# A graph-attention layer on one core: a sixth pair's rows gathered from x, and four moves in the schedule

## The chip, the core and the metric

The kernel runs on one core of a Trainium2 chip. The metric is the device time of one execution in microseconds. A core has five engines that work through their own instruction streams: TensorE (PE; its weight loads are shown as PEld), VectorE (DVE), ScalarE (ACT), GpSimd (POOL) and SyncE (SP). They wait for each other by semaphores. Here SP issues nearly all plain transfers, POOL issues the gathers, and ACT issues a few loads of edge attributes.

## The reference

For 12500 nodes and 400000 edges, sorted by target node `dst`, all in float32:

```python
h = relu(layernorm(x))                                  # 12500 x 128
msg_src = h @ w_src + b_src;  msg_dst = h @ w_dst
message = msg_src[src] + msg_dst[dst]                   # 400000 x 128
rad = silu(silu(edge_attr @ w1 + b1) @ w2 + b2) @ w3 + b3   # 32 -> 64 -> 64 -> 128
message = message * edge_weight * rad
message = message @ w_sep + b_sep                       # 128 -> 256: 8 heads x (16 alpha, 16 value)
alpha = 0.6*a + 0.4*a*(2*sigmoid(a) - 1)                # a: the alpha half
score = sum over k of alpha * alpha_dot                 # one per edge and head
att = softmax of score over the edges of each target
out = segment_sum(value * att, dst) @ w_proj + b_proj
return x + out
```

## The kernel before

**Node phase** (some 110 us). The 98 tiles of 128 rows of x are held in SBUF and handled in quads of four tiles. A first loop over 25 quads makes the layer norm, the transposes (`turn`) and the product with `w_src`, and stores the table `t_src` in DRAM. A second loop (28 rounds in both versions) makes the product with `w_dst` (`products(i, 1)`) and stores the table `t_dst`. Both tables wait for copies from PSUM by ACT, and SP stores them. Into the second loop other work is laid by round number (`extra`): `spans`, `cuts`, `direct_ids`, `spreads`, and four `marks` (L601, DVE), which compare neighbouring targets and end with four stores to `same`. SP takes one load of weights or of first edge data per round from a list (`weights_list`).

**Raw sections.** A section is 512 edges, a pair of sections is 1024 edges, and there are 391 pairs. `t_src` can be gathered from only once it is whole. So for the first `RAW` pairs POOL gathers rows of x itself (`raw_gather`, L381), right at the start; in the second loop these rows get their own statistics (`raw_roots`, L390), layer norm (`raw_norm`, L406 and L408), transposes and relu (`raw_turn`, L416), a quad of four tiles at a time, and later PE multiplies them by `w_src` (`sources`, L1169) instead of turning gathered rows of `t_src` (L1173).

**Windows phase** (the rest). The scheduling is by hand: each engine runs its instructions in the order in which the Python code emits them. `step(k)` for k = -5 to 390 issues stages of several pairs at once:

- loads on SP: the target rows `md` of pair k+4 (`load_md`, L1080), `dst` (`load_d`, L187), edge weights of pair k+2 (`load_w`, L194); edge attributes on ACT's queue for the first pairs, then on SP's (L175)
- `split_md(k+1, 0)` on ACT (L1090) and `split_md(k+1, 1)` on DVE (L1094): the target rows of the pair, made into the stationary operand of `message`
- `alphas(k-1, f)`, f = 0 and 1: PE (L1197), then a Silu on ACT (L1199), then `alphas_sum` on DVE (L1204)
- `sources(k, f)` on PE, `gather(k+2, f)` on POOL (L1111: four gathers of 128 rows, eight per pair)
- the radial network: `mlp1(k+2)` (PE L1127, two Silu on ACT L1130, out of half of the bank `misc` and half of the bank `m`), `mlp2(k+1)` (PE L1140, ACT L1142), `mlp3(k)` (PE L1157) and `radial(k)` (DVE L1162)
- `one_hot_T(k+1)`: two ACT instructions (L1151, L1152) make the one-hot matrix of the targets
- `message(k)`: PE (L1186), then DVE (L1191) writes `mT`, the product with `rad`
- every second step `scores` of two pairs (PE L1214, into the bank `m`)
- from step 8 on, the softmax of eight pairs, spread over steps: at k % 8 == 3 an Exp on ACT (`softmax_exp`, L1250, with a table load before it and one before the next Silu), the copy S (L1218) and two rounds of transposes with ACT copies into `Pem` (`softmax_T`, L1284, L1287)
- from step 12 on (`LAG`) the values of pair k-12 (PE L1325, DVE L1327), the one-hot sums (L1340, L1352) and their stores.

Buffers: `mT` and `early` are one ring of 13 pairs. In the node phase slots 10, 11 and 12 of it hold the first edge weights, the first `dst` rows and the second edge weights; slots 0 to 4 hold raw rows; gathers of pairs 5 to 12 go into `early`, pair 10 only when `message(0)` has used the weights there. Pairs 13 to 18 have six buffers `gs`, pair 19 borrows two others, pair 20 takes the buffer of pair 13 again, and from pair 26 on each pair takes that of six pairs before. `padded_rows` loads four blocks of x, adds a bias and stores them, one half per step in steps 40 to 47.

Of the kernel before, what the change touches and what calls it, by code (L numbers as in the profile page):

```python
# [43 lines left out]
MP = 8  # L44
MQ = 2 * MP
LAG = 12
RAW = 5
# [10 lines left out]
def gnn_kernel(ctx: ExitStack, tc: tile.TileContext, a: dict, out: bass.AP):  # L58
# [139 lines left out]
    with tc.tile_pool(name="node1", bufs=1) as n1, tc.tile_pool(name="node", bufs=2) as np_, \  # L198
# [80 lines left out]
        def weights_list():  # L279

            pairs = []
            first = ("heads", "dot", "b_v", "w_proj", "b_proj", "b_a")
            for name, t in sorted(wt.items(), key=lambda v: v[0] not in first):
                ap = a[name]
                if name == "b_src":
                    ap = ap.rearrange("o c -> c o")
                elif name == "b_proj":
                    ap = ap.to_broadcast([P, C])
                pairs.append((t, ap))
            for f in range(2):  # L290
                for q in range(2):
                    o = (2 * q + f) * RAD
                    pairs.append((w1b[o:o + RAD, f * FC:(f + 1) * FC], a["fc_w1"]))
                s = slice(f * FC, (f + 1) * FC)
                for q in range(2):
                    pairs.append((w2b[s, q * FC:(q + 1) * FC], a["fc_w2"]))
                pairs += [(w3b[s, :], a["fc_w3"]), (b12[s, 0:1], a["fc_b1"]), (b12[s, 1:2], a["fc_b2"])]
            return [lambda t=t, ap=ap: nc.sync.dma_start(out=t, in_=ap) for t, ap in pairs] + \
                [lambda k=k: load_e(k, nc.sync) for k in range(4)] + \
                [lambda: load_d(0, early[AHEAD - 2].bitcast(I32).rearrange("p (n e) -> p n e", n=2)),  # L300
                 lambda: load_w(0, early[AHEAD - 3]), lambda: load_w(1, early[AHEAD - 1])]
# [336 lines left out]
        roots(quads[3][0], quads[4][1])  # L638
        more = iter(weights_list())
        limits = load_limits()  # L640
        for i in range(Q):
# [31 lines left out]
            if i == 19:  # L673
                ends_load()
        extra = {7: lambda: (spans(), places()), 10: cuts, 12: direct_ids, 14: spreads,
                 15: lambda: marks(0), 16: lambda: marks(1), 18: lambda: marks(2), 20: lambda: marks(3)}
        for i in range(2 * RQ + 8):
            if i < Q:
                products(i, 1)
            if i % 2 == 0 and 0 <= i // 2 - 4 < RQ:  # L680
                raw_turn(i // 2 - 4)
            q = i // 2 - 1
            if i % 4 == 2 and q < RQ:
                raw_roots(q, q + 2)
            if i % 4 == 3 and q < RQ:
                raw_scales(q, q + 2)
            if i % 2 == 0 and 0 <= q - 1 < RQ:
                raw_norm(q - 1)
# [5 lines left out]
            if i == 2 * RQ:  # L694
                nc.scalar.activation(silu, eps[0:1, :], AF.Silu)
# [313 lines left out]
    def windows():  # L1009
# [7 lines left out]
        with tc.tile_pool(name="ps", bufs=1, space=PSUM) as pp, \  # L1017
# [104 lines left out]
            def mlp1(k):  # L1122
# [6 lines left out]
                for f in (1, 0):  # L1129
                    nc.scalar.activation(h1s[k][:, f, :], p1[f], AF.Silu, bias=b12[:, 0:1], scale=1.0)  # L1130
# [510 lines left out]
            for k in range(2):  # L1641
                load_md(k)

# [20 lines left out]
            def step(k):  # L1664
# [31 lines left out]
                if 0 <= k - 40 < 8:  # L1696
                    padded_rows(k - 40)
# [10 lines left out]
                if has(k + 1) and k >= 0:  # L1708
                    split_md(k + 1, 0)
# [3 lines left out]
                if k == NP:  # L1713
                    tail_head(c)
                    return
                if has(c):
# [12 lines left out]
                if has(k + 1) and k >= 0:  # L1729
                    split_md(k + 1, 1)  # L1730
# [9 lines left out]
                if has(k + 2):  # L1740
                    mlp1(k + 2)
                if has(k + 1):
                    one_hot_T(k + 1)
                if has(k):
                    radial(k)
                if k == 0:
                    for i in range(2):
                        split_md(0, i)
# [30 lines left out]
                if has(k + 2):  # L1779
                    gather(k + 2, 1)  # L1780
                if has(k + 3):
# [11 lines left out]
                if has(k):  # L1793
                    message(k)
                if has(k - MP) and r == 3:
# [230 lines left out]
```

## Time and profile before

| | us |
|---|---|
| median of 3 runs | 4045.88 |
| lowest, highest | 4044.23, 4051.89 |
| the profiled execution | 4045.58 |
| its span, first to last instruction | 4043.7 |
| PE busy | 3734.2 |
| POOL busy | 3015.5 |
| DVE busy | 2966.2 |
| ACT busy | 2317.5 |

A row of the timeline gives the start and the duration in us, the engine, the line of the code, the operation, output and input, the count, and in brackets the idle time of the engine before it with what ended it. A row of the groups gives line, engine, operation, shapes and count, then busy time and mean ns of one, then the idle time before them and what ended most of it. A row of the windows gives busy time (and instructions) of PE, PEld, DVE, ACT and POOL, then the granted clock, the busy share of the DMA engines and GB/s. POOL's time between two gathers is not booked as busy: issuing instructions do not count. The mean granted TensorE clock was 0.974.

### The profile page before, as it was taken

The page shows a single profiled execution, that of the slowest core. Times are in us where ns is not written, and L with a number is a line of the kernel's source. Part 1 is how long each engine was busy: PE and PEld are TensorE (multiplying, and loading weights), DVE is VectorE, ACT ScalarE, POOL GpSimd, SP SyncE. Part 2 cuts the span into 40 slices and gives each one's busy share as a digit, 9 for nine tenths or more (in the row PEclk, how much of TensorE's full clock was granted, in tenths as well). Part 3 has the DMA queues.
Part 4 walks back from the last instruction along what each step waited for, and adds up shares of the span by engine and source line. Part 5 has one row for each costly group of instructions (what it writes and reads, how often), then busy time and mean ns, then how long its engine had stood idle before and what let it go on. Part 6 is the DMA issues. An engine that isn't in the chain of part 4 may idle for free. (4 is left out here: it accounts for less than half of the span.)

```text
span 4043.7 us, 82719 instructions
## 1 busy us (share of the span) xinstructions
PE 3734.2 (92%) x27186; PEld 2198.2 (54%) x27186; DVE 2966.2 (73%) x5236; ACT 2317.5 (57%) x4463; POOL 3015.5 (75%) x3193
## 2 busy tenths in 40 slices
PE   7699999999999999999999999999999999999997
PEld 6255555555555555555555555555555555565555
DVE  8477777777777767677777677777777777777876
ACT  7565555666655556555655565555555555555561
POOL 6767777777777777777777777777777777777776
PEclk9899999999999999999999999999999999999998
DMA  8756666666666665665566666666666666666662
GB/s 256 189 154 166 166 177 170 162 171 170 175 160 170 167 162 159 166 162 166 158 169 169 163 164 169 168 162 165 172 171 159 178 167 180 174 179 181 174 166 56
DMA packets 435839, 678.82 MB, mean 168 GB/s; under 512 B 96574, under 2 KB 268510, under 8 KB 435291
## 3 DMA queue, kind: packets, MB, share of 16 engines
q1 hardware_dynamic: 331931, 464.59, 39.4%
q0 software_dynamic: 101888, 207.34, 21.8%
q8 instruction: 220, 3.60, 0.4%
q14 instruction: 216, 1.77, 0.2%
q10 hardware_dynamic: 1584, 1.51, 0.1%
HBM read 620.73 MB, written 54.06 MB: 167 GB/s over the span
## 5 line engine op out<-in xcount | busy, mean ns | idle before, releaser
L1111 POOL DMA_INDIRECT gs<-t_src,idx x3013 | 2849.4, 946 | 932.4 <-issue 757.2
L1204 DVE SCALAR_TENSOR_TENSOR al<-pa,sl 128x512 f32<-128x512 f32 x781 | 538.9, 690 | 544.1 <-ACT sl L1199 533.2
L1197 PE MATMUL pa<-mT,c_w_a 128*128 128x512 f32 x1562 | 884.1, 648 | 38.7 <-DVE mT L1191 17.9
L1199 ACT ACTIVATE sl<-pa,c_b_a 128x512 f32<-128x512 f32 x781 | 536.8, 687 | 666.4 <-PE pa L1197 659.5
L1325 PE MATMUL V<-c_w_v,mT 128*128 128x128 f32 x6154 | 891.2, 288 | 11.4 <-DVE pvx L1327 10.7
L1325 PEld LDWEIGHTS V<-c_w_v,mT 128*128 128x128 f32 x6154 | 757.3, 194 | 240.9 <-issue 186.3
L1173 PEld LDWEIGHTS pm<-ident,gs 128*128 128x128 f32 x3013 | 374.5, 143 | 536.3 <-issue 526.3
L1142 ACT ACTIVATE h<-p,b 128x512 f32<-128x512 f32 x391 | 467.7, 1196 | 345.7 <-PE p L1140 339.5
L1327 DVE TENSOR_TENSOR pvx<-V,Pem 128x512 f32<-128x512 f32 x770 | 528.0, 686 | 146.4 <-PE V L1325 96.9
L1162 DVE SCALAR_TENSOR_TENSOR w_b<-p,c_fc_b,w_b 128x1024 f32<-128x1024 f32 x389 | 498.2, 1281 | 147.1 <-PE p L1157 119.7
L1173 PE MATMUL pm<-ident,gs 128*128 128x128 f32 x3013 | 464.3, 277 | 99.5 <-DMA gs<-t_src,idx 98.9
L1191 DVE SCALAR_TENSOR_TENSOR mT<-pm,c_b_src,w_b 128x1024 f32<-128x1024 f32 x389 | 495.6, 1274 | 14.8 <-PE pm L1186 14.5
L1130 ACT ACTIVATE h<-misc,b 128x256 f32<-128x256 f32 x391 | 185.6, 475 | 540.7 <-PE misc L1127 522.4
L1157 PE MATMUL p<-h,w3b 64*128 64x512 f32 x1564 | 454.9, 659 | 8.0 <-ACT h L1142 8.0
L1197 PEld LDWEIGHTS pa<-mT,c_w_a 128*128 128x128 f32 x1562 | 236.2, 191 | 288.3 <-issue 78.7
L1214 PE MATMUL m<-al,w_s 128*32 128x512 f32 x1564 | 215.8, 623 | 80.8 <-ACT h L1130 79.6
L1152 ACT ACTIVATE ohT<-d_b,ones 128x512 fp32r<-128x512 f32 x389 | 280.8, 722 | 13.0
L1151 ACT ACTIVATE d_b<-d_b,tgt 128x512 f32<-128x512 int32 x389 | 279.9, 719 | 0.0
L1140 PE MATMUL p<-h,w2b 64*64 64x256 f32 x3128 | 260.3, 403 | 0.0
L1127 PEld LDWEIGHTS m<-eT,w1b 64*128 64x128 f32 x782 | 151.0, 193 | 196.6 <-issue 169.9
L1127 PE MATMUL m<-eT,w1b 64*128 64x256 f32 x782 | 239.5, 387 | 3.9 <-DMA t_dst<-ms 2.7
L1127 PE MATMUL misc<-eT,w1b 64*128 64x256 f32 x782 | 239.5, 387 | 0.0
(257 smaller groups left out, 3730.3 us busy)
## 6 DMA issues: line engine op xcount, KB each, us to landing
w_b<-in_edge_weight SPq DMA_DIRECT2D x388, 512.0 KB
d_b<-in_dst SPq DMA_DIRECT2D x388, 256.0 KB
e_t<-in_edge_attr SPq DMA_DIRECT2D x381, 128.0 KB
gs<-t_src,idx POOLq DMA_INDIRECT x3013
md<-t_dst SPq DMA_DIRECT2D x782, 32.0 KB
win<-ob SPq DMA_DIRECT2D x230, 68.0 KB
agg<-ob SPq DMA_DIRECT2D x640, 16.5 KB
xs<-in_x SPq DMA_DIRECT2D x26, 256.0 KB
```

The source lines that it names most:

```text
L1111: sent = [nc.gpsimd.indirect_dma_start(out=gs[:, t, :], out_offset=None, in_=t_src[:, :], in_offset=bass.IndirectOffsetOnAxis(ap=idx[:, t0 ...
L1127: nc.tensor.matmul(p1[f], w1b[s, :], eTs[k][s, :], start=True, stop=True)
L1142: nc.scalar.activation(h2s[k].rearrange("x (h i b) -> x h b i", h=2, b=2 * TS), p2[:, :, 0:2 * T].rearrange("x h (b i) -> x h b i", b=2 * TS),
L1157: nc.tensor.matmul(p3[:, f, 0:SEC], w3b[s, :], h2s[k][s, :], start=True, stop=True)
L1162: nc.vector.scalar_tensor_tensor(rad[:, 0:n], p3.rearrange("c f e -> c (f e)")[:, 0:n], b3, rad[:, 0:n], op0=ALU.add, op1=ALU.mult)
L1173: turned = [nc.tensor.matmul(pm[:, t * T:(t + 1) * T], gs[:, t, :], ident, start=(t == 0), stop=False, is_transpose=True, skip_group_check ...
L1191: nc.vector.scalar_tensor_tensor(mTs[k][:, 0:n], pms.rearrange("c f e -> c (f e)")[:, 0:n], b_n, rad[:, 0:n], op0=ALU.add, op1=ALU.mult)
L1197: nc.tensor.matmul(pa[:, 0:n], w_a, mTs[k][:, f * SEC:f * SEC + n], start=True, stop=True)
L1199: nc.scalar.activation(sl[:, 0:n], pa[:, 0:n], AF.Silu, bias=b_a, scale=1.0)
L1204: nc.vector.scalar_tensor_tensor(al, pa, 0.25, sl, op0=ALU.mult, op1=ALU.add)
L1325: nc.tensor.matmul(V[:, t, :], mTs[c][:, o:o + T], w_v, start=True, stop=True)
L1327: nc.vector.tensor_mul(pvx[c][:, f, 0:n, 0:C].rearrange("p t (h k) -> p t h k", h=H), V[:, 0:n, :].rearrange("p t (h k) -> p t h k", h=H), ...
```

## The change

1. `RAW` is 6 instead of 5: 48 raw gathers instead of 40, 12 raw quads instead of 10, and 8 gathers from `t_src` fewer.
2. The raw work of a round becomes a function `raw_rows`. Its first four rounds run in the last four rounds of the first loop, beside the four `marks`, which move there too from rounds 15 to 20 of the second loop. The second loop keeps its 28 rounds.
3. The second pair's edge weights are no longer in the list of the node phase: `load_w(1)` is issued by SP behind the first two `load_md`.
4. In step 0 the target rows of pair 0 are split at the usual place, and those of pair 1 behind `message(0)`; before, pair 1 came first.
5. `one_hot_T(k+1)` moves behind the second alphas, sources and gathers of its step, in every step.
6. In steps with k % 8 == 3 from 11 on, `mlp1(k+2)` moves to the same place, so that it is behind the second alphas. For odd pairs below 320 its two Silu change order.
7. The eight halves of `padded_rows` are spread over steps 40 to 51.

```diff
-RAW = 5
+RAW = 6
@@ weights_list
-                 lambda: load_w(0, early[AHEAD - 3]), lambda: load_w(1, early[AHEAD - 1])]
+                 lambda: load_w(0, early[AHEAD - 3])]
@@ node phase
+        def raw_rows(i):
+            if i % 2 == 0 and 0 <= i // 2 - 4 < RQ:
+                raw_turn(i // 2 - 4)
+            q = i // 2 - 1
+            if i % 4 == 2 and q < RQ:
+                raw_roots(q, q + 2)
+            if i % 4 == 3 and q < RQ:
+                raw_scales(q, q + 2)
+            if i % 2 == 0 and 0 <= q - 1 < RQ:
+                raw_norm(q - 1)
...
+            if 0 <= i - (Q - 4) < 4:
+                marks(i - (Q - 4))
+                raw_rows(i - (Q - 4))
-        extra = {7: lambda: (spans(), places()), 10: cuts, 12: direct_ids, 14: spreads,
-                 15: lambda: marks(0), 16: lambda: marks(1), 18: lambda: marks(2), 20: lambda: marks(3)}
-        for i in range(2 * RQ + 8):
+        extra = {7: lambda: (spans(), places()), 10: cuts, 12: direct_ids, 14: spreads}
+        for i in range(2 * RQ + 4):
             if i < Q:
                 products(i, 1)
...
+            raw_rows(i + 4)
...
-            if i == 2 * RQ:
+            if i == 2 * RQ - 4:
                 nc.scalar.activation(silu, eps[0:1, :], AF.Silu)
@@ mlp1
-                for f in (1, 0):
+                for f in (0, 1) if k % 2 and k < KV else (1, 0):
@@ before the steps
             for k in range(2):
                 load_md(k)
+            load_w(1, early[AHEAD - 1])
@@ step
-                if 0 <= k - 40 < 8:
-                    padded_rows(k - 40)
+                if 0 <= k - 40 < 12 and (k - 40) % 3 != 1:
+                    padded_rows((k - 40) // 3 * 2 + (k - 40) % 3 // 2)
...
-                    split_md(k + 1, 0)
+                    split_md(k + (k > 0), 0)
...
+                after = has(k - MP) and r == 3 and k < NP
...
-                    split_md(k + 1, 1)
+                    split_md(k + (k > 0), 1)
...
-                if has(k + 2):
+                if has(k + 2) and not after:
                     mlp1(k + 2)
-                if has(k + 1):
-                    one_hot_T(k + 1)
                 if has(k):
                     radial(k)
-                if k == 0:
-                    for i in range(2):
-                        split_md(0, i)
...
                 if has(k + 2):
                     gather(k + 2, 1)
+                if has(k + 2) and after:
+                    mlp1(k + 2)
+                if has(k + 1):
+                    one_hot_T(k + 1)
                 if has(k + 3):
                     e_T(k + 3)
...
                 if has(k):
                     message(k)
+                if k == 0:
+                    for i in range(2):
+                        split_md(1, i)
```

9 lines of the change are left out of this document (removed).

## The prediction

> **What bounds the kernel now.** I read the groups by shape first, then the windows, the gaps on POOL's timeline, and only then the waits of the other engines.
>
> ```profile
> L1111 POOL DMA_INDIRECT gs<-t_src,idx x3013 | 2849.4, 946 | 932.4 <-issue 757.2 <-PE pm L1173 44.4 <-DMA gs<-t_src,idx 39.0
> 2000.00:3000.00 1000.00, 924.00 (x6801) 535.74 (x6799) 730.57 (x1250) 577.01 (x1096) 756.43 (x800) 0.98 0.62 166
> PE m L1214 <- ACT h L1130: 79.6, 45, 2.9
> ```
>
> PE looks like the bound (924 of 1000 us busy). But in the same 1000 us POOL issues 800 gathers, one every 1.25 us: 0.95 busy and 0.30 before the next, which the first row books as "issue". A pair needs 8 gathers, so POOL takes 10.0 us a pair and is never free. Where it does rest, its timeline shows:
>
> ```profile
> 59.40 0.95 POOL L381 DMA_INDIRECT mT<-in_x,idx  x1 [0.30 <-issue]
> 72.19 0.94 POOL L1111 DMA_INDIRECT mT<-t_src,idx  x1 [11.84 <-DMA c_fc_b<-in_fc_b]
> ...
> 97.91 1.86 POOL L1111 DMA_INDIRECT mT<-t_src,idx  x1 [0.30 <-issue]
> ...
> 123.79 0.94 POOL L1111 DMA_INDIRECT mT<-t_src,idx  x1 [0.30 <-issue]
> 129.77 0.94 POOL L1111 DMA_INDIRECT mT<-t_src,idx  x1 [5.03 <-DVE mT L1191]
> ...
> 237.32 0.94 POOL L1111 DMA_INDIRECT gs<-t_src,idx  x1 [7.98 <-PE pm L1173]
> ...
> 303.39 0.94 POOL L1111 DMA_INDIRECT gs<-t_src,idx  x1 [6.38 <-PE pm L1173]
> ...
> 3950.24 0.94 POOL L1111 DMA_INDIRECT gs<-t_src,idx  x1 [0.30 <-PE misc L1352]
> ```
>
> Four rests: for the stored t_src (11.84 us), for message(0), which frees the buffer that pair 10 goes into (5.03), and twice for PE to be done with the rows six or seven pairs back: pair 20 waits for step 13 (7.98), pair 26 for step 20 (6.38). No later rest is longer than an issue gap. The edges make 400000 / 128 = 3125 gathers; from pair 26 on, 3125 - 26 x 8 = 2917 run at (3950.24 - 303.39) / 2916 = 1.2506 us, and 93 us of tail follow. So the end is the time of step 20's `sources` plus a constant 3740 us, and a change counts for what it does to that time. The 79.6 us that PE waits on ACT in 45 exponent steps are nearly all behind this gate and cost nothing.
>
> **The change part by part.** The sum has four terms ahead of the gate: the stores of t_dst, step 0, steps 1 to 10, step 11.
>
> *The sixth raw pair.* POOL makes 8 gathers more before t_src and 8 fewer after. The first 48 end near 59.40 + 0.95 + 8 x 1.25 = 70.4, inside the 11.84 us of rest; the 32 for pairs 6 to 9 then end near 115 instead of 124.7. Alone this is worth 0: POOL would wait 15 us for message(0) instead of 5. It only makes room for an earlier message(0).
>
> *Node phase.* Its end decides when the last t_dst stores land, since `load_md` waits for them:
>
> ```profile
> 93.52 0.68 DVE L416 TENSOR_SCALAR mT<-pt 128x512 f32<-128x512 f32 x1
> 94.12 1.42 DVE L390 BATCH_NORM_STATS2 mvr<-mT 128x6 f32<-128x256 f32 x4
> 95.45 0.33 DVE L408 TENSOR_SCALAR h<-mT,rstdr,shiftr 128x128 f32<-128x128 f32 x1
> 97.87 1.08 DVE L601 TENSOR_TENSOR gt<-cur 112x896 bf16<-112x896 int32 x1
> ...
> 98.98 0.88 SPq L605 DMA_DIRECT2D same<-gt  x2
> 106.04 1.12 SPq L194 DMA_DIRECT2D mT<-in_edge_weight  x1
> 108.06 0.75 SPq L369 DMA_DIRECT2D t_dst<-ms  x1
> 117.17 6.64 SPq L1080 DMA_DIRECT2D md<-t_dst  x6
> ```
>
> and, from the windows and from the list of DMA issues:
>
> ```profile
> 98.00:116.00 18.00, 9.25 (x37) 4.79 (x35) 4.42 (x8) 6.37 (x15) 14.04 (x14) 0.60 0.96 296
> ...
> mT<-in_edge_weight SPq DMA_DIRECT2D x2, 512.0 KB
> same<-gt SPq DMA_DIRECT2D x1, 672.0 KB
> same<-gt SPq DMA_DIRECT2D x1, 105.0 KB
> ```
>
> From 98 to 116 the DMA engines are 96% busy at 296 GB/s, and the md loads start at 117.17, when the t_dst stores have landed. The change takes the marks' stores (672 + 105 KB) and one weight load (512 KB) out of that stretch: 1289 KB / 296 GB/s = 4.4 us. On DVE the second loop loses four marks (4 x 1.08 = 4.3) and the first statistics (1.42) and gains two quads (half of 1.42, 0.33 and 0.68 each, together 3.4): 2.3 us less, which I give to the copies that feed those stores, since ACT norms each raw quad between them. Together -6.7. SP's lag behind the copies (last store issued at 108.06) goes with it, as the four stores of marks and the weight load no longer stand ahead. The price is in the first loop: marks and statistics put 5.7 us on DVE there, with ACT's root behind them, and four stores on SP ahead of the first t_dst stores and weights. That can delay t_src by about 2 us; POOL's 15 us ahead of message(0) cover it, and without that cover it would cost those 2 us. Bounds: -10 (all of SP's lag is won beside the transfers), -3 (only the transfers, less 1.5 us of delay).
>
> The marks have a price on POOL too: the gather beside the mark at 97.87 took 1.86 instead of 0.94. The marks now stand beside raw gathers, whose last eight may end up to 4 x 0.92 = 3.7 us later, near 74; the same cover hides it. The Trainium skill (SBUF — State Buffer, "SBUF: two separate sides", the box on SWDGE) says that a two-port VectorE operation locks GpSimd out while it writes descriptors; by that, moving the marks beside the raw gathers moves the stall and removes none, and the trace agrees with 1.86 against 0.94. The Trainium skill (DMA: Bandwidth & Descriptors, "Anatomy of one DMA") gives a fixed 2.0 us and 436 GB/s for a DMA, measured on the gpsimd path; as an estimate from those figures a 512 KB store lands in 3.2 us, not in the 9 us between 108.06 and 117.17, and this term would be beyond -10; the trace does not agree while its queue is full.
>
> *Step 0.*
>
> ```profile
> 124.44 0.40 ACT L1090 ACTIVATE m<-md,sign 128x128 fp32r<-128x128 f32 x1 [4.00 <-DMA md<-t_dst]
> 126.84 0.39 ACT L1090 ACTIVATE m<-md,sign 128x128 fp32r<-128x128 f32 x1
> 128.21 1.28 DVE L1191 SCALAR_TENSOR_TENSOR mT<-pm,c_b_src,mT 128x1024 f32<-128x1024 f32 x1 [0.24 <-PE pm L1186]
> 133.17 0.40 ACT L1090 ACTIVATE m<-md,sign 128x128 fp32r<-128x128 f32 x1 [3.15 <-DMA d_b<-in_dst]
> ```
>
> Today md(1) is split first (124.44) and md(0) 2.4 us later, behind two Silu and the one-hot. Now md(0) comes first: up to -2.4. Against it, load_w(1) now stands on SP behind md(1), about 1 us ahead of md(2), the index rows and dst, and step 1 waits at 133.17 for just such a dst load. Bounds -2.4 and +2; I take 0, because 133.17 is the later row and lies on SP's queue.
>
> *Steps 2 to 10: one-hot behind the second alphas.* These steps have no values yet, and PE waits for mT in each.
>
> ```profile
> 176.84 1.12 PE L1197 MATMUL pa<-mT,c_w_a 128*128 128x512 f32 x2
> 178.43 0.72 ACT L1152 ACTIVATE ohT<-d_b,ones 128x512 fp32r<-128x512 f32 x1
> 179.06 0.67 ACT L1199 ACTIVATE sl<-pa,c_b_a 128x512 f32<-128x512 f32 x1
> 181.70 1.12 PE L1197 MATMUL pa<-mT,c_w_a 128*128 128x512 f32 x2 [2.29 <-DVE mT L1191]
> 185.70 1.06 PE L1214 MATMUL m<-al,w_s 128*32 128x512 f32 x8 [0.94 <-ACT h L1130]
> ...
> 220.13 0.47 ACT L1130 ACTIVATE h<-misc,b 128x256 f32<-128x256 f32 x1
> 220.50 0.47 ACT L1130 ACTIVATE h<-m,b 128x256 f32<-128x256 f32 x1
> ```
>
> In the even step the alphas are ready at 176.84 + 1.12 = 177.96, but their Silu starts at 179.06 behind the one-hot; it feeds al, mT and the next step. Moved, it saves 1.1 in each of steps 2, 4, 6, 8, 10. In odd steps the scores wait 0.94 for the bank that the second Silu reads; in the new order that Silu is first, 220.50 - 220.13 = 0.37 sooner: four steps, 1.5. Sum 7.0; the one-hot now delays the second layer's Silu and SP may feed steps 2 and 3 late, so I take -5.5 (bounds -7 and -2). From step 12 on PE has the values to do and is the slower one, so the same move brings 0.
>
> *Step 11 (first exponent step).*
>
> ```profile
> 218.83 1.28 ACT L1130 ACT_TABLE_LOAD   x1
> 221.02 1.84 PE L1214 MATMUL m<-al,w_s 128*32 128x512 f32 x8 [2.94 <-ACT h L1130]
> 222.91 0.69 ACT L1218 ACTIVATE S<-m,b_s 128x512 f32<-128x512 f32 x1 [0.58 <-PE m L1214]
> 226.06 0.37 ACT L1287 COPY Pem<-misc 128x256 f32<-128x256 f32 x1 [0.54 <-PE misc L1284]
> 226.54 0.44 PE L1284 MATMUL misc<-ident,Pr 128*128 128x128 f32 x2
> 226.82 1.06 PE L1325 MATMUL V<-c_w_v,mT 128*128 128x128 f32 x8
> ```
>
> The first layer now follows the second alphas, so the scores no longer wait 2.94 us for its Silu, and the exponent's second table load falls behind S. ACT then runs exp (to 218.83), S 0.69, table load 1.28, Silu 0.67, the first layer's two (0.37 + 0.47), the one-hot (1.4) and the Pem copy 0.37: 224.1, where the second transposes start today at 226.54. Saves 2.4 (bounds 0 and -4). From step 19 on, PE puts the values ahead of the scores, and the same chain ends within 0.2 us of today's; past the gate it is worth nothing anyway.
>
> *The rest.* `split_md` after step 0 and the order of the first layer's Silu past step 11 lie under POOL's 10.0 us a pair. The spread of `padded_rows` over steps 40 to 51 removes DVE waits for x behind the gate: 0; its cover is POOL's pace, and if that were gone it would be a gain.
>
> **Sum.** -6.7 + 0 - 5.5 - 2.4 = -14.6 us. Can POOL follow? It goes from pair 10 to pair 26 in 128 x 1.25 = 160 us; today it takes 303.39 - 129.77 = 173.6, with the two rests. The steps give 7.9 of those 13.6 back, so pair 20's rest goes nearly to nothing and pair 26 still waits for PE. The profiled execution took 4045.58 us (span 4043.7 and 1.9 around it): 4031.0; the median of the runs, 4045.88, is 0.3 above it, which is less than I can tell: 4031.
>
> **Rivals.**
> *The node phase ends no earlier.* The marks and the first statistics (5.7 us) are only moved within a DVE that is the busy one there, and the marks' stores now stand ahead of the t_dst stores, whose buffers ACT waits for. Then the first term is 0 and only the steps' 7.9 remain: 4038. For it: the first loop's roots stand on ACT ahead of its copies. Against: the stretch from 98 to 116 is full, and 1289 KB leave it.
> *SP feeds steps 0 to 4.* load_w(1) lands before ACT may go on, step 0 pays +2 and the light steps save only 2: -6.7 + 2 - 2 - 2.4 = -9.1, 4036.5. For it: the wait at 133.17. Against: later light steps show no such wait.
> *Slower: the step becomes longer than POOL's 10.0 us.* The one-hot (1.4 us) now stands right ahead of the second layer's Silu, which the next step's third layer needs. PE is busy 9.24 us of 10.0 per pair, so nothing happens up to 0.76 us more a step; from there each 0.1 us over 365 steps costs 36 us: at 0.1 us beyond it 4031 + 36 = 4067. Against it: ACT is busy only 577 of 1000 us, and the next third layer comes after the values, alphas and transposes of its step.
> *More.* With 1289 KB out of the way the last stores find a nearly empty queue and land as the md loads do in the idle stretch behind (issued from 117.17, waited for until 124.44, with six of them in between), so that SP's whole lag is won, and md(0) first brings its 2.4: -10 - 2.4 - 7 - 3 = -22.4: 4023. That is the way in which the figures of the Trainium skill (DMA: Bandwidth & Descriptors, quoted above) point. Against: d, w(0) and two t_dst stores still meet there. POOL's 160 us is the floor of the steps' part.
> That the change does not do what it says is the case of the sixth pair itself: alone it gives 0.
>
> **How the numbers follow.** Forecast (4026 to 4036) 0.57; node phase no earlier 0.17; SP 0.10; more 0.08; slower 0.08. 0.2% is 8.1 us (about what a measurement of this kernel can tell from no change), so faster means under 4037.8: the forecast, "more", most of SP's case and half of the first rival, 0.77; same 0.15; slower 0.08. The range leaves out the slow case and the tails: 4023 to 4041.
>
> **What would show it.** Right: pair 10's first gather (the one that waits for mT) starts near 123 instead of 129.77; the md loads near 110.5; pair 20's gather without a rest; pair 26's near 289, its rest still there but shorter; from there to the last gather 3647 us as now, and the same tail. In the even light steps PE's wait for mT (2.29 at 181.70) is about 1.1 us shorter. Wrong: md loads still near 117 (first term); the 133.17 wait as far behind them as now or farther (SP); gather waits on PE or gaps over 0.35 us after pair 26, or gathers over 1.25 us apart (the constant was none).

## The result and the profile after

| | before | after |
|---|---|---|
| median of 5 runs, us | 4047.99 | 4031.61 |
| ratio, 95% interval | | 0.9961 (0.9948 to 0.9973) |
| the profiled execution | 4045.58 | 4031.61 |
| its span | 4043.7 | 4029.8 |

The change makes the kernel 16.4 us faster by the medians and 13.9 us by the two spans; 4031 was forecast. (The median before is now taken over five executions, not three.) The timeline of the kernel after, rows of five engines in order of time (six lines more than before stand ahead of the steps' code, so L1111 is now L1117 and L1080 is L1086):

```profile
59.08 1.69 POOL L381 DMA_INDIRECT mT<-in_x,idx  x1 [0.30 <-issue]
...
64.09 1.08 DVE L601 TENSOR_TENSOR gt<-cur 112x896 bf16<-112x896 int32 x1
72.70 1.11 POOL L1117 DMA_INDIRECT mT<-t_src,idx  x1 [0.30 <-issue]
...
103.30 0.87 ACT L359 COPY ms<-pm 128x512 f32<-128x512 f32 x3
105.82 0.71 SPq L369 DMA_DIRECT2D t_dst<-ms  x1
112.17 0.94 POOL L1117 DMA_INDIRECT mT<-t_src,idx  x1 [0.30 <-issue]
113.85 4.08 SPq L1086 DMA_DIRECT2D md<-t_dst  x4
120.02 0.40 ACT L1096 ACTIVATE m<-md,sign 128x128 fp32r<-128x128 f32 x1 [2.74 <-issue]
122.28 1.24 DVE L1197 SCALAR_TENSOR_TENSOR mT<-pm,c_b_src,mT 128x1024 f32<-128x1024 f32 x1
123.79 0.94 POOL L1117 DMA_INDIRECT mT<-t_src,idx  x1 [10.68 <-DVE m L1100]
128.15 0.69 ACT L1205 ACTIVATE sl<-pa,c_b_a 128x512 f32<-128x512 f32 x1 [0.22 <-PE pa L1203]
132.59 0.72 ACT L1157 ACTIVATE d_b<-d_b,tgt 128x512 f32<-128x512 int32 x1 [3.76 <-DMA d_b<-in_dst]
...
173.89 1.12 PE L1203 MATMUL pa<-mT,c_w_a 128*128 128x512 f32 x2 [1.24 <-DVE mT L1197]
223.87 0.94 POOL L1117 DMA_INDIRECT gs<-t_src,idx  x1 [0.30 <-issue]
288.21 0.94 POOL L1117 DMA_INDIRECT gs<-t_src,idx  x1 [4.70 <-PE pm L1179]
...
3937.58 0.94 POOL L1117 DMA_INDIRECT gs<-t_src,idx  x1 [0.30 <-issue]
```

POOL now goes from the raw rows to `t_src` with no rest (72.70; it rested 11.84 us), is done with pair 9 at 113.1 and waits 10.68 us for message(0) ahead of pair 10 (5.03 before). Pair 20 starts at 223.87 with no rest, pair 26 at 288.21 after a rest of 4.70 instead of 303.39 after 6.38. From there to the last gather it is 3649.4 us, as against 3646.9. So the whole gain stands at 288.21 already (15.2 us), POOL gives 2.5 back later and the tail gains 1.2: 13.9, as the spans say.

Where the 15.2 us come from is read off the start of DVE's write of `mT` in each step (us, L1191 before and L1197 after), for these two kernels and for the experiments told below:

| kernel | step 0 | 2 | 10 | 12 | 18 | 20 | pair 26's first gather |
|---|---|---|---|---|---|---|---|
| before | 128.2 | 146.2 | 213.7 | 234.2 | 287.7 | 309.2 | 303.4 |
| after | 122.3 | 139.2 | 203.0 | 220.6 | 274.1 | 294.0 | 288.2 |
| without the step moves | 123.6 | 146.1 | 217.1 | 238.7 | 292.2 | 312.1 | 306.3 |
| the step moves alone | 126.8 | 142.9 | 208.0 | 225.5 | 279.1 | 299.0 | 293.2 |
| without the step moves, with useless matmuls | 121.9 | 141.9 | 215.6 | 238.8 | 292.3 | 312.2 | 306.4 |
| five raw pairs | 123.1 | 140.8 | 204.8 | 222.4 | 275.9 | 295.8 | 290.0 |

The windows of the kernel after:

```profile
98.00:116.00 18.00, 9.19 (x42) 4.36 (x40) 3.56 (x7) 8.94 (x21) 11.46 (x13) 0.65 0.80 250
2000.00:3000.00 1000.00, 924.38 (x6783) 537.28 (x6781) 728.49 (x1248) 561.50 (x1088) 756.66 (x799) 0.98 0.62 167
```

and its waits (total us, times, longest us):

```profile
PE misc L1290 <- ACT h L1136: 39.3, 42, 1.2
PE misc L1290 <- ACT Pem L1293: 32.2, 49, 1.0
...
POOL gs L1117 <- PE pm L1179: 26.2, 71, 4.7
```

In the steady state nothing has changed: PE 924.4 of 1000 us (924.0 before), 799 gathers (800). Of the 79.6 us that PE waited for ACT ahead of the scores 2.2 are left, and two rows of 39.3 and 32.2 us ahead of the softmax transposes stand there instead: in the exponent steps the wait was moved 71.5 us' worth, not removed. PE's wait for gathered rows to land grew from 98.9 to 116.8 us, as it should where POOL is the bound.

### The profile page after: what moved, and what is told of

Its sections match the earlier page's. It is cut to its first block, busy times and chain, and to the rows that moved or that the text cites. A ratio compares the mean times of both kernels' runs of the same rounds, so it can differ in the third digit from the quotient of the medians.

```text
span 4029.8 us, 82612 instructions
## 1 busy us (share of the span) xinstructions
PE 3727.2 (92%) x27190; PEld 2199.6 (55%) x27190; DVE 2971.6 (74%) x5246; ACT 2277.0 (57%) x4470; POOL 3018.5 (75%) x3193
## 5 line engine op out<-in xcount | busy, mean ns | idle before, releaser
L1117 POOL DMA_INDIRECT gs<-t_src,idx x3013 | 2852.4, 947 | 922.7 <-issue 766.4
L1203 PE MATMUL pa<-mT,c_w_a 128*128 128x512 f32 x1562 | 874.1, 642 | 30.8 <-DVE mT L1197 11.8
L1179 PE MATMUL pm<-ident,gs 128*128 128x128 f32 x3013 | 459.3, 275 | 117.5 <-DMA gs<-t_src,idx 116.8
L1197 DVE SCALAR_TENSOR_TENSOR mT<-pm,c_b_src,w_b 128x1024 f32<-128x1024 f32 x389 | 496.0, 1275 | 16.2 <-PE pm L1192 15.2
L1136 ACT ACTIVATE h<-m,b 128x256 f32<-128x256 f32 x391 | 183.6, 469 | 158.6 <-PE misc L1133 151.6
```

What stands on the lines that cost most here:

```text
L1117: sent = [nc.gpsimd.indirect_dma_start(out=gs[:, t, :], out_offset=None, in_=t_src[:, :], in_offset=bass.IndirectOffsetOnAxis(ap=idx[:, t0 ...
L1179: turned = [nc.tensor.matmul(pm[:, t * T:(t + 1) * T], gs[:, t, :], ident, start=(t == 0), stop=False, is_transpose=True, skip_group_check ...
L1197: nc.vector.scalar_tensor_tensor(mTs[k][:, 0:n], pms.rearrange("c f e -> c (f e)")[:, 0:n], b_n, rad[:, 0:n], op0=ALU.add, op1=ALU.mult)
L1203: nc.tensor.matmul(pa[:, 0:n], w_a, mTs[k][:, f * SEC:f * SEC + n], start=True, stop=True)
```

## The experiments

Five of the runs below, like those of the two versions, are on chips on which the kernel before takes about 4046 us (called the usual chips below); the other seven fell on chips on which it took 5622 and 5536 us, and on which POOL itself waits for PE for 876 to 1074 us. They are told together at the end.

**Is POOL the bound, and are its rests all there is to win?** Seven buffers instead of six, and slot 10 free from the start:

```diff
-GSB = 6
+GSB = 7
-al = sp.tile([C, SEC], F32, name="al", bufs=6)
+al = sp.tile([C, SEC], F32, name="al", bufs=5)        # rx 2 -> 1, two ob 5 -> 4
-                 lambda: load_w(0, early[AHEAD - 3])]
+                 lambda: load_w(0, early[AHEAD - 1])]
-            load_w(1, early[AHEAD - 1])
+            load_w(1, lp.tile([P, PR], F32, name="w_b", bufs=3))
```

> The changed kernel with seven buffers gs instead of six (room made by five instead of six buffers al, one instead of two rx, four instead of five ob), the second pair's edge weights in a w_b buffer, and the first pair's in ring slot 12, so that slot 10 is free from the start and pair 10 waits for nothing. Theory: both rests of POOL that are left in the changed kernel (10.7 us ahead of pair 10, 4.7 ahead of pair 26) go. Pair 10 starts at 113.4, pair 21 at 223.5 (step 13's sources end then), pair 28, which now takes the buffer of pair 21, waits for step 21's sources, which end at 296.9 in the changed kernel: pair 28 at 297 instead of 308.3, so 11 us faster than the changed kernel, 4020.5. Rival A, PE sets the time and POOL's rests are only slack: 4031.6, the rests come back elsewhere. Rival B, gathers at 113 to 123 hold up the last stores of t_dst and the first md loads, or five buffers al cost a wait in every second step: 4032 or more.

Measured: 4019.25 us, ratio to before 0.9937 (0.9923 to 0.9950). Its timeline:

```profile
115.39 0.94 POOL L1117 DMA_INDIRECT mT<-t_src,idx  x1 [0.30 <-issue]
122.35 0.40 ACT L1096 ACTIVATE m<-md,sign 128x128 fp32r<-128x128 f32 x1 [3.87 <-DMA w_b<-in_edge_weight]
...
298.59 0.94 POOL L1117 DMA_INDIRECT gs<-t_src,idx  x1 [3.67 <-PE pm L1179]
...
3927.24 0.94 POOL L1117 DMA_INDIRECT gs<-t_src,idx  x1 [0.30 <-issue]
```

The rest ahead of pair 10 is gone (pair 10 starts at 115.39), so is that ahead of pair 26, and one of 3.67 us is left ahead of pair 28, at 298.59 instead of 308.3. PE's steps are no faster here (step 20 at 295.4 against 294.0), and still the kernel is 12.4 us faster than the one after: it is POOL that sets the time, and its rests that are to be won. The forecast was 4020.5. This version is faster than both kernels.

**Is the sixth raw pair worth something by itself?**

```diff
-RAW = 6
+RAW = 5
-        for i in range(2 * RQ + 4):
+        for i in range(max(Q, 2 * RQ + 4)):
```

> The changed kernel with RAW = 5: 40 raw gathers, ten raw quads, the second loop as long as the 25 quads need (25 rounds instead of 28). Theory: the sixth pair alone is worth 0. POOL's gathers up to pair 9 end 10 us later, at 122, which is still ahead of message(0) (pair 10's first gather at 123.8 in the changed kernel); pair 26 waits for step 20 as before it. The shorter second loop may bring message(0) forward by up to 2 us. So pair 10 at 122 to 124, pair 26 at 286 to 288.2, time 4029.5 to 4031.6. Rival, the rows gathered sooner are what carries the gain: POOL is behind by the 10 us of eight gathers, pair 26 at 298, time 4041.

Measured: 4032.82, ratio to before 0.9968 (0.9956 to 0.9980). Pair 10 starts at 124.62 after a rest that is 2.77 instead of 10.68, pair 26 at 290.00:

```profile
124.62 0.95 POOL L1117 DMA_INDIRECT mT<-t_src,idx  x1 [2.77 <-DVE m L1100]
...
290.00 0.94 POOL L1117 DMA_INDIRECT gs<-t_src,idx  x1 [4.77 <-PE pm L1179]
```

Against the kernel after that is +1.2 us, which cannot be told from none; pair 26 came 1.8 later, not up to 2 sooner as the shorter loop allowed. The eight gathers only change how long POOL waits for message(0). The rival (4041) falls.

**What are the step moves worth?** They were undone in the kernel after, and done alone in the kernel before:

```diff
 # without the step moves (from the kernel after)
-                for f in (0, 1) if k % 2 and k < KV else (1, 0):
+                for f in (1, 0):
...
-                if has(k + 2) and not after:
+                if has(k + 2):
                     mlp1(k + 2)
+                if has(k + 1):
+                    one_hot_T(k + 1)
...
-                if has(k + 2) and after:
-                    mlp1(k + 2)
-                if has(k + 1):
-                    one_hot_T(k + 1)
```

> The changed kernel with its step moves undone: the one-hot stands again ahead of the first layer's place, the first layer stands at its old place in exponent steps, and its two Silu are in the old order. All else (node phase, sixth raw pair, load_w(1), the split of step 0) stays changed. Theory (POOL's gathers are the bound, and only the time of step 20's sources counts): the trace of the changed kernel puts 4.8 us on steps 1 to 10, 2.9 on steps 11 and 12 and 1.6 on step 19, so pair 26's first gather comes 9.3 us later, at 297.5 instead of 288.2, and the time is 4041. By the terms of the prediction (5.5 + 2.4) it would be 296.1 and 4039.5. Rival A, the gain all comes from the node phase: 288.2 and 4031.6. Rival B, PE is the bound and the 45 exponent steps count: some 80 us slower, 4110.

> The kernel before with only the step moves: the one-hot behind the second alphas, the first layer behind them in exponent steps, its Silu order. Five raw pairs, the old node phase, the old split, load_w(1) in the node phase. Theory: pair 10's first gather stays at 129.8, and pair 26's comes 9.3 us sooner than before, at 294.1 (7.9 by the prediction's terms: 295.5); time 4038.5. POOL could have had pair 26 at 129.8 + 160 = 289.8, so the old start of POOL is no limit. Rival A, the moves bring nothing without the earlier rows: 303.4 and 4047.9. Rival B, PE is the bound: 80 us faster, 3968.

Measured: without the moves 4047.33, ratio to before 1.0002 (0.9993 to 1.0011); the moves alone 4036.85, 0.9975 (0.9966 to 0.9984). The moves alone do what was expected (pair 26 at 293.2; 294.1 expected). Without them the whole node phase, the sixth pair and the split bring nothing at all, and pair 26 comes later than before; 4041 had been expected. So the parts do not add up: the same moves are worth 10.2 us at pair 26 on the old start and 18.1 on the new one. By the table above, the 18.1 are 1.3 at step 0, 5.7 in steps 1 and 2, 7.1 in steps 3 to 10, 4.1 in steps 11 and 12 and nothing from there on; the 10.2 are 1.4, 1.9, 2.4 and 2.9 in the same places and 1.6 from step 18 to step 20. The timeline without the moves shows where it begins:

```profile
114.21 4.09 SPq L1086 DMA_DIRECT2D md<-t_dst  x4
125.07 0.94 POOL L1117 DMA_INDIRECT mT<-t_src,idx  x1 [12.25 <-DVE m L1100]
...
132.69 0.72 ACT L1157 ACTIVATE d_b<-d_b,tgt 128x512 f32<-128x512 int32 x1 [1.86 <-DMA d_b<-in_dst]
134.07 0.67 ACT L1205 ACTIVATE sl<-pa,c_b_a 128x512 f32<-128x512 f32 x1
135.38 1.27 DVE L1197 SCALAR_TENSOR_TENSOR mT<-pm,c_b_src,mT 128x1024 f32<-128x1024 f32 x1
136.71 2.08 PE L1203 MATMUL pa<-mT,c_w_a 128*128 128x512 f32 x2 [3.83 <-DVE rf L1062]
...
299.54 1.06 PE L1220 MATMUL m<-al,w_s 128*32 128x512 f32 x8 [1.86 <-ACT h L1136]
300.53 1.12 PE L1203 MATMUL pa<-mT,c_w_a 128*128 128x512 f32 x2
306.32 0.94 POOL L1117 DMA_INDIRECT gs<-t_src,idx  x1 [4.81 <-PE pm L1179]
```

In step 1 ACT comes to the one-hot of pair 2 before its `dst` rows have landed, and waits for them to 132.69. With the old order the second alphas' Silu stands behind that (134.07); in the kernel after it stands ahead (128.15), and only the second layer's Silu waits. So the message of step 1 starts at 135.38, PE has idled 3.83 us, and then the two alphas matmuls take 2.08 instead of 1.12. The steps start 4.7 us sooner than before, and at step 2 all of that is lost (146.1 against 146.2).

**And the clock.** The granted clock in these stretches, by the windows; without the step moves:

```profile
136.00:140.00 4.00, 3.29 (x4) 1.18 (x4) 1.76 (x6) 0.69 (x1) 2.83 (x3) 0.50 1.03 222
```

in the kernel after:

```profile
136.00:140.00 4.00, 3.68 (x20) 1.27 (x16) 3.67 (x5) 2.97 (x6) 2.83 (x3) 1.00 0.94 220
```

and in the kernel before, in steps 11 and 19:

```profile
220.00:224.00 4.00, 2.98 (x10) 0.85 (x11) 0.00 (x0) 2.97 (x6) 3.09 (x4) 0.65 0.51 122
296.00:300.00 4.00, 4.00 (x18) 1.88 (x18) 1.15 (x2) 1.61 (x3) 0.94 (x1) 0.57 0.48 135
```

The timeline of the kernel before, with its last copies for `t_dst` and the matmuls of these two steps:

```profile
102.68 0.87 ACT L359 COPY ms<-pm 128x512 f32<-128x512 f32 x3
...
222.79 2.00 PE L1197 MATMUL pa<-mT,c_w_a 128*128 128x512 f32 x2
295.04 1.07 PE L1214 MATMUL m<-al,w_s 128*32 128x512 f32 x8 [1.86 <-ACT h L1130]
296.03 1.88 PE L1197 MATMUL pa<-mT,c_w_a 128*128 128x512 f32 x2
```

TensorE falls to half its clock for 3.4 us, or for twice that, after it has waited. Behind message(0) the kernel before has such a dip in steps 1, 11 and 19, the kernel without the moves has them in steps 1, 3, 9 and 11, and in the trace of the kernel after there is none up to pair 26. Step 19 is the cleanest reading: before, and without the step moves, the order is the same and PE waits the same 1.86 us for the first layer's Silu. Before, the next two alphas take 1.88 and steps 18 to 20 take 21.5 us; without the moves they take 1.12 and 19.9 us, as in the kernel after (19.9). So the first layer's move by itself is worth 0 there, and the 1.6 us are the clock's. In step 11 the dip stretches the scores (1.84, in the prediction; 1.07 at full clock) and the alphas (2.00; 1.13): 1.6 of the 2.9 us gained in steps 11 and 12.

Why the same wait of 1.86 us brings a dip in one kernel and none in the other can be read from finer windows. In windows of 0.1 us, the clock of the kernel before falls at 129.0, 221.2 and 296.3 and rises again 3.4 us later each time; without the moves it falls at 124.7, 135.0, 148.6, 199.8 and 223.7 and rises at 128.1, 141.8, 152.0, 203.2 and 230.5. In each trace these times lie whole multiples of 3.41 us apart (from 129.0 to 296.3 it is 49 times that), as if stretches of that length ran on regardless of the kernel. The stretches around step 19, in the kernel before:

```profile
292.90:296.30 3.40, 1.54 (x12) 0.51 (x11) 2.09 (x5) 3.35 (x6) 2.49 (x4) 1.00 0.52 104
296.30:299.70 3.40, 3.40 (x10) 1.50 (x9) 0.85 (x2) 1.31 (x3) 0.71 (x1) 0.50 0.41 105
```

and without the step moves:

```profile
295.40:298.80 3.40, 2.28 (x16) 1.36 (x12) 3.26 (x6) 3.35 (x4) 2.62 (x3) 1.00 0.31 56
298.80:302.20 3.40, 2.66 (x16) 1.13 (x16) 0.84 (x3) 3.09 (x6) 2.10 (x3) 1.00 0.44 112
```

Before, the whole wait falls into one stretch, in which PE is busy 1.54 us, and the next one runs at half clock. Without the moves a border cuts the wait in two, and neither stretch is idle enough. Over the seven traces on usual chips, from the clock's first rise behind the node phase (at 120.6 to 125.6) to pair 26, all nine stretches at full clock with PE busy for 1.54 us or less were followed by a dip and none with 1.91 or more; of the six between, two were. The borders lie at other times in each trace and follow no instruction. Of the three traces with the old order the dip of step 19 came in one and that of step 11, where PE waits longer, in all three; so the first is luck as far as these traces show, and the second belongs to the order.

The Trainium skill (TensorE: Matmul & The Clock Gate, "The HAM clock gate") says that the array runs at half rate after an idle window of about 3.4 us and at full rate after as much work. The traces agree with the half (0.50 in the window, 2.08 against 1.12) and with the length (each dip lasts 3.4 us or twice that). They do not show that PE has to be idle for so long: a dip followed stretches in which it was busy for 1.54 of 3.41 us.

Would the clock alone have given the 18.1 us back? Ten useless matmuls at the end of each of steps 0 to 11 keep PE busy:

```diff
                     mlp2(k + 1)
+                if 0 <= k < LAG:
+                    for t in range(10):
+                        nc.tensor.matmul(pv[:, t % TS, :], w_a, w_v, start=True, stop=True, ...)
```

> The kernel without the step moves (the one at 4047.3, whose pair 26 starts at 306.3) with ten more 128x128 matmuls on PE at the end of each of steps 0 to 11, into the bank that nothing else uses before step 12: about 1.5 us of useless work a step, 18 us in all, put where PE waits for mT. Clock theory: what undoing the moves cost there (18.1 us against the changed kernel, twice the 9.3 forecast) is half the moves' own worth and half the TensorE clock, which falls to 0.5 when PE has idled for some us; between 120 and 230 the matmuls of that kernel took 15.6 us longer than at full clock, those of the changed kernel none. The useless work keeps the clock up, so pair 26 starts at 294 to 298 and the time is 4035 to 4039. Not all dips go, since the wait in step 1 lies elsewhere. Rival, the waits themselves are the cost and the clock only shows them: pair 26 at 306 or later, time 4047 or more.

> The same kernel as the one with useless matmuls, on another chip, since on the chip of the second call even the kernel before took 5622. As before: without the step moves pair 26 starts at 306.3 and the time is 4047.3. Clock theory: with ten useless 128x128 matmuls at the end of each of steps 0 to 11 the clock stays up, pair 26 starts at 294 to 298, time 4035 to 4039. Rival, the waits themselves are the cost: 306 or later, 4047 or more.

Measured on a usual chip: 4047.42, ratio 1.0001 (0.9992 to 1.0010), pair 26 at 306.4. The windows of that run:

```profile
136.00:140.00 4.00, 4.00 (x15) 1.47 (x13) 2.33 (x3) 2.18 (x5) 3.08 (x4) 1.00 0.98 230
```

and its timeline:

```profile
131.03 2.50 PE L1809 MATMUL V<-c_w_v,c_w_a 128*128 128x128 f32 x20
134.95 1.13 PE L1203 MATMUL pa<-mT,c_w_a 128*128 128x512 f32 x2 [1.41 <-DVE rf L1062]
```

The clock does stay up (1.00 where it was 0.50; the only dip left is at 224.4), and nothing is won at pair 26. At step 2 this kernel is 4.2 us ahead of the same one without useless work (141.9 against 146.1), 1.7 of them from step 0, and by step 12 it has lost them again: steps 3 to 10 take 73.7 us instead of 71.0, without a dip. The useless work was mis-sized, 2.50 us a step instead of 1.5, and by these figures stands on the path itself. So the run by itself does not decide how much of the 18.1 us the clock carries.

Part of it can be read elsewhere. In steps 3 to 10 the kernel without the moves and the kernel before issue the same work in the same order, and the first takes 71.0 us where the second takes 67.5. The 3.4 us between them are what two dips of 3.4 us at half clock cost, and the first has two there (148.6, 199.8), the second none: 3.0 of the 3.4 us arise in steps 3 and 9, in which the dips lie. With the 2.5 us that the useless work won in steps 1 and 2, about 6 of the 18.1 us are the clock's, as an estimate from these figures; how the rest splits between the wait in step 1, ACT's order and the dips stays open.

**Seven runs that decide nothing.** On these chips engines stood still for stretches that the profile only books as "remote". Of the waits in the second run of the old traffic:

```profile
POOL gs L1117 <- PE pm L1179: 976.0, 244, 62.8
ACT h L1136 <- remote: 360.1, 70, 27.6
```

POOL waited 976 us for PE there, against 26.2 in the kernel after, so the time of step 20 no longer sets the end, on which these expectations rest. The edits, beside the useless matmuls on such a chip (5613.51, ratio 0.9971, 0.9936 to 1.0006): the marks and load_w(1) back in the second loop (5578.42, ratio 0.9899, 0.9851 to 0.9946, on one chip and 5511.70, 0.9974, 0.9943 to 1.0005, on another);

```diff
-                marks(i - (Q - 4))
+        extra = {..., 15: lambda: marks(0), 16: lambda: marks(1), 18: lambda: marks(2), 20: lambda: marks(3)}
+                 lambda: load_w(0, early[AHEAD - 3]), lambda: load_w(1, early[AHEAD - 1])]
```

> The changed kernel with the four marks and their stores back in rounds 15 to 20 of the second loop, and load_w(1) back in the list of the node phase; six raw pairs, their early rounds and all step moves stay. By the prediction's first term (1289 KB at 296 GB/s) the md loads start 4.4 us later than the changed kernel's 113.9, at 118.2, and pair 26 at 292.6: 4036. By the trace of the changed kernel the node phase ended only 3.3 sooner than before, and the second loop now has two raw quads more on DVE than before, so I take md loads at 117 to 118, pair 26 at 291.5 to 292.5, time 4035 to 4036. Rival A, the traffic was not on the path (ACT's copies, which end at 104 in both, were): 113.9 and 4031.6. Rival B, a later start lets the clock fall in steps 0 to 11: pair 26 later by clearly more than the md loads, 4039 or more.

> The same as the kernel with the old traffic in the second loop, on a chip at its usual speed. As before: by the prediction's first term the md loads start at 118.2 instead of 113.9, pair 26 at 292.6, time 4036; I take 117 to 118, 291.5 to 292.5, 4035 to 4036. Rival A, the traffic is not on the path: 113.9 and 4031.6. Rival B, a later start lets the clock fall in steps 0 to 11: 4039 or more.

the last of the eight gathers left out in every pair from 26 on, so that its tile keeps older rows and the output is not the layer's, in the kernel before (one execution, 4933.36) and after (one execution, 5036.58);

```diff
-                    for t in range(tiles(k, f))]
+                    for t in range(min(tiles(k, f), TS - f if k > 25 else TS))]
```

> The kernel before with seven gathers instead of eight for every pair from 26 on (the last tile of the pair keeps the rows that its buffer held). Theory: POOL then needs 8.75 us a pair, less than PE, whose steps from 20 to 40 take 9.29 on average, exponent steps included; so PE sets the end: 309.2 + 370 x 9.29 + 84 after the last mT = 3830, 217 faster. Rival, PE is already the bound: no change, 4046.

> The changed kernel with the same seven gathers of eight from pair 26 on. Its steps from 20 to 40 take 9.13 us on average: 294.0 + 370 x 9.13 + 84 = 3756, so 74 faster than the kernel before with seven (15 from the start, 59 from the exponent steps and the rest). So the moves in the steps would be worth some 75 us, and POOL hides all but 15 of it. Rival A, the exponent steps' moves are worth nothing in the steady state in any case: 15 faster than the kernel before with seven. Rival B, PE is the bound: 4032.

the `dst` rows of pairs 2 and 3 loaded earlier, without the step moves (5514.97, 0.9986, 0.9946 to 1.0027), and in the version with more buffers, with ACT's loads at the end of a step (5502.52, 0.9974, 0.9937 to 1.0012):

```diff
+            load_d(1, lp.tile([P, 2, SEC], I32, name="d_b"))   # behind load_w(1)
-                if k % 2 and k >= -1 and has(k + 3):
+                if k % 2 and k >= 1 and has(k + 3):
 # the version with more buffers, besides: behind mlp2(k + 1) instead of at the start of the step
+                if has(k + 6) and 4 <= k + 6 < AHEAD:
+                    load_e(k + 6, nc.scalar)
```

> The kernel without the step moves (4047.3, pair 26 at 306.3), and the dst rows of pairs 2 and 3 loaded by SP right behind load_w(1) instead of in step -1, behind the md of pairs 2 and 3. Theory, an interaction: with the one-hot at its old place ACT waits in step 1 for these rows (to 132.69) ahead of the second alphas' Silu (134.07; 128.15 in the changed kernel), PE idles 3.83 us, its clock falls to 0.5 and the next matmuls take 2.08 instead of 1.13; so undoing the moves cost 18.1 and not 9.3. With the rows there in time the second Silu comes at about 129 to 130 and pair 26 at 298 to 301: time 4039 to 4042. Rival A, the loss lies in the order of ACT in the later steps: 305 or later, 4046 or more. Rival B, the earlier dst load takes the queue from md(2) and w(2), which become the wait: 303 to 306, 4044 to 4047.

> The kernel with seven buffers gs and slot 10 free (4019.3, pair 28 at 298.6), with two moves in the first steps: the dst rows of pairs 2 and 3 loaded right behind load_w(1), and the edge attributes that ACT loads issued at the end of a step, not at its start, where that issue waited for an older transfer and held md(0) until 122.35. Theory: the end follows the time of step 21's sources, down to POOL's own floor, pair 10 at 115.4 + 144 x 1.2506 = 295.5 for pair 28. Step 0 comes 2 to 3 us sooner and step 1 another 1 to 2, so POOL's floor decides: pair 28 at 295.5, 3.1 sooner, time 4016. Rival, the gate is not in these steps: 4019.3 or, if the loads collide, more.

With seven gathers of eight the kernel before took 4933 us where it took 5622 with all, so gathers weigh on these chips too, although POOL also waits. The changed kernel came out 103 us slower than the one before there, where 74 faster was expected; with one execution of each, nothing follows from that.

So three things were not settled: what of the node phase is the traffic's, whether an earlier load of the `dst` rows frees step 1, and what the steps are worth with POOL out of the way.

## Why the prediction was right, step by step

The time (4031 forecast, 4031.61 measured) and the frame were right; the terms were less so. The node phase brought 3.4 us less than forecast, and step 0 (2.6 us) and the clock in step 19 (1.6 us), both put at 0 in it, made up for most of it. That pair 26 comes within 0.6 us of the forecast is luck; that it comes some 15 us sooner and that the whole gain stands there is what the prediction had understood.

| term | forecast, us (bounds) | measured, us |
|---|---|---|
| node phase | -6.7 (-10 to -3) | -3.3 |
| step 0 | 0 (-2.4 to +2) | -2.6 |
| steps 1 to 10 | -5.5 (-7 to -2) | -4.7 |
| steps 11 and 12 | -2.4 (0 to -4) | -2.9 |
| step 19 | within 0.2 of none | -1.6 |
| pair 26's gather | -14.6 | -15.2 |
| behind it, tail included | 0 | +1.3 |

- *POOL's gathers are the bound, and only the time of step 20's `sources` counts*: right. The signs promised on POOL came: pair 10 at 123.79 (near 123), pair 20 without a rest, pair 26 at 288.21 (near 289) with a shorter one. The constant of 3740 holds to 1.3 us (2.5 on POOL, at 1.2515 us a gather instead of 1.2506, less 1.2 in the tail), and no rest behind pair 26 is longer than 0.45 us until the tail. The version with more buffers shows the same from the other side.
- *The sixth pair alone is worth 0*: right, +1.2 without it.
- *Node phase*: mis-sized by half. The md loads start at 113.85, not near 110.5. The 4.4 us of transfers were taken as if the stretch from 98 to 116 had no other limit. Its DMA share did fall, from 0.96 to 0.80. But the 2.3 us of relief for DVE never reached the copies: the last end at 104.2 (103.30 and 0.87) as against 103.6 before (102.68 and 0.87). The last store of t_src is issued as early as before (69.25 and 69.27), so the 2 us of delay feared there did not come, but the first store of t_dst is issued at 73.94 instead of 70.89: with the marks and statistics ahead of it the second loop starts 3 us later. What was won is SP's lag (the last store issued at 105.82 instead of 108.06) and 1.1 us of landing. Over all seven traces on the usual chips the md loads start at 112.7 to 115.1 with the new node phase (five kernels) and at 116.9 and 117.2 with the old one, 3.0 between the means. What of this is the traffic's stays open.
- *Landing*: the last store is issued at 105.82 and the md loads go at 113.85, 8.0 us later, with the share of the DMA engines at 0.80. The prediction took the store at 108.06 for one of 512 KB; by the DMA issues the last one has 42 KB, the one before it 64 KB, and the last of 512 KB is issued at 105.60 before and from 104.85 after. The Trainium skill's fixed 2.0 us and 436 GB/s (DMA: Bandwidth & Descriptors, "Anatomy of one DMA") give, as an estimate, 3.2 us for 512 KB and 2.1 us for 42 KB; the trace does not agree, with 1289 KB less in the queues either.
- *Step 0*: taken at 0 because the dst load seemed to be the later lane. It gave 2.6, a little beyond the bound, and the reason was wrong for the kernel with the moves: ACT still waits for a dst load, in step 1 (132.59, 3.76 us), but the one-hot that waits now stands behind the second alphas. By the means of all seven traces (md loads to `mT` of step 0: 9.0 against 10.5) the step is worth 1.5.
- *SP feeds steps 0 to 4*, a rival at 0.10: the wait is real, and without the one-hot's move it eats the whole gain of the node phase. The prediction treated the terms as a sum; they are a sum only because the one-hot's move covers this wait.
- *Even light steps*: right. PE's wait for mT at 173.89 is 1.24, 1.05 less than the 2.29 before, and step pairs from 4 to 10 take 15.2 to 15.7 instead of 16.7, 3.9 us together. Steps 1 and 2 gave 1.1, one clock dip in the kernel before among them, and steps 3 and 4 lost 0.2.
- *Step 11, step 19*: the step that failed is that the clock was taken as given: of the rows shown for step 11 the scores (1.84 us) run at half clock. Each step has 1.6 us of clock dip before and none after; without it step 11 gave 1.3 and not 2.4, and step 19 the forecast 0. In step 11 the change took away the wait that brings the dip, in step 19 the dip hung on where the stretches of 3.41 us lay.
- *The marks' price on POOL* was moved and not removed, as forecast: a raw gather beside the marks takes 1.69 us (59.08), those of pairs 6 to 9 now 1.11 (72.70) to 1.27 at the start and 0.94 later (112.17).
- *Slower, the step longer than POOL's 10.0 us*: did not come; PE 924.4 of 1000 us as before.
- *The chances*: the parts named for faster (0.57, 0.08, most of 0.10 and half of 0.17) make about 0.8, a little more than the 0.77 given.

## What to carry to other kernels

Find the engine whose instructions follow each other without a rest, list its few rests, and ask of each part of a change only what it does to those; the 71.5 us that moved within the exponent steps were worth nothing, and one more buffer with one slot freed was worth 12. Terms in front of such a gate do not add when they share a queue: undo each part in the changed kernel as well as doing it alone, since a wait that one part uncovers may be covered by another. Where a path holds an engine that idles, compare the durations of the same instruction before and after, since the clock may have moved with the schedule, or by luck alone.

## What the hardware showed that was not expected

- In these traces TensorE's clock changes only at borders that lie 3.41 us apart, and halves for one or two such stretches after one in which PE was busy for about half of it or less (always at 1.54 us or less, never at 1.91 or more). So a wait of 1.86 us may bring a dip or not, and one dip cost 1.6 us on the path. There is one profile for each kernel; whether the borders move from one execution of a kernel to the next is not shown.
- ACT's own issue of a load seems to wait for an older transfer and to hold the work behind it: in the version with more buffers ACT issues a load at 121.84 and splits md(0) at 122.35, after 3.87 us that by the profile end with the landing of the second edge weights; in the kernel after the split is at 120.02, after 2.74 us for which the profile names no transfer. That the issue is what waits is inferred; the version that moved those loads ran only on a slow chip.
- On some chips the kernel before took 5536 to 5622 us instead of 4046, with gathers as long as elsewhere (0.95 us in the mean) and long waits that the profile books only as "remote". The cause is open.
